# Gathering the first 28 edge tiles from x instead of z, in a graph layer followed by a mixture of experts

## The chip, the core and the metric

The kernel runs on one core of a Trainium2 chip. The metric is the device time of one execution in microseconds (us), and lower is better. The engines are named as the profile names them: PE (TensorE, matmuls), PEld (its weight loads), DVE (VectorE), ACT (ScalarE), POOL (GpSimd) and SP (SyncE). SP and ACT also issue plain transfers, and POOL issues the indirect ones (gathers).

## What is computed

There are 6250 nodes with 256 features, 100,000 edges sorted by destination, and 8 experts with 512 hidden units. Cut to what matters:

```python
def gnn(h, src, dst, W, b):                 # h = layernorm(x)
    msg_sum = segment_sum(h[src], dst)      # one row of h for each edge, summed by destination
    deg = segment_sum(ones, dst)
    agg = msg_sum / maximum(deg, 1)[:, None]
    return concatenate([h, agg], axis=1) @ W.T + b

def ffn(h, ...):                            # h = layernorm(x) of the new x
    xn = layernorm(h) * gamma + beta
    logits = xn @ Wr + br                   # 8 experts, the best 2 of each node are used
    y = sum over the two: softmax weight * (gelu(xn @ W1[e] + b1[e]) @ W2[e] + b2[e])

x = x + gnn(layernorm(x), src, dst, W, b)
x = x + ffn(layernorm(x), ...)
```

## The kernel before

**Weights first, then edges.** The kernel does not sum normalised rows and multiply the sums by W. It multiplies each node row first: `z` is layernorm(x) times the second half of W, with 8 router columns beside it (264 columns, `DZ`), and `u` is x plus the bias plus layernorm(x) times the first half. Both go to device memory (`z_d`, `u_d`). The mean is folded into the weights (`center_weights`, giving `gc`), so a row needs only a product with `gc` and a scale by its own `rstd_x`.

**z stage.** The 49 node tiles of 128 rows are taken in blocks of 4 (`TB`). `load_block` loads x both as rows (`xt`, for the statistics) and as columns (`x_t`, for the products), four blocks ahead. `z_block` takes a block two tiles at a time: `product` makes two PSUM tiles on PE, ACT scales them into `zt` (L284), and SP stores the block in `z_d` (L287). After each pair of tiles it runs one piece of the list `ahead`, which is the statistics of two later node tiles on DVE (`statistics`: L184 and L185), every fourth piece with the deviations of eight tiles (`z_deviations`: a root on ACT and five small DVE instructions). It also runs one entry of the list `steps`. Before the change `steps` has nine entries from block 5 on: constants, the windows of destinations (`place_windows`, `spread_windows`, `place_rows`, `check_windows`), and two checks that the destinations are sorted (`check_order`, L310 and L311).

**u stage.** `u_stages` gives 26 closures. The first 25 each make u of two node tiles: a load of x rows (`xu`, L197), an addition on DVE (L376), two products on PE (L260), four DVE instructions (L383 and L384) and, one closure later, a store (L388).

**Edge stage.** The edges are cut into 784 tiles of 128, 14 tiles (`C`) to a window and 56 windows (`W`). For a tile, POOL gathers 128 rows of `z_d` by `src_i` into one of 28 buffers (`XG`, `xg`), L566, and PE adds them by destination with a one-hot matrix made on DVE (`hot`, L577) into the PSUM tile `pS` (L583). The gather of tile t + 28 is issued behind the matmul of tile t. When a window is complete, `window_done` plans what follows at later tiles: a row that two windows share is passed on by way of device memory (`shared_row`, L589; `keep_sums`, `put_sums`, `share_row`), `window_x1` makes the new x from u and the sums, and after each group of four windows the router, the sorting of tokens and the experts' matmuls are laid between the later edge tiles.

**Order.** Every engine's instructions stand in the order in which the program writes them. `at(t, f)` puts a step behind edge tile t. Before the change six u closures run ahead of tile 0, and the others behind the even tiles 0 to 38. When the last of them has run, the memory of u is freed, the cleared expert inputs (`clear_slots`, L828) and the 16 weight loads on ACT's queue follow. One entry of `loads` (19 in all: expert biases and zeros for device memory, L1094) goes out with each tile from tile 0 on.

Of the kernel before, what the change touches and what calls it, by code (L numbers as in the profile page):

```python
# [17 lines left out]
P = 128  # L18
# [7 lines left out]
GB = 3  # L26
LATE = 40
XG = 28


@with_exitstack
def gnn_ffn_kernel(ctx: ExitStack, tc: tile.TileContext, x, x_cols, src, dst, dst_next, gw, gw_t, gb, gb_cols, gamma, beta,
                   wr, br, w1, b1, w2, b2, out):

# [123 lines left out]
    lanei = early.tile([P, 1], I32, name="lanei", bufs=1)  # L158
    nc.gpsimd.iota(lanei, pattern=[[1, 1]], base=0, channel_multiplier=1)

    def constants():
        nc.vector.tensor_scalar(before, ej, 0.0, None, op0=ALU.is_lt)
        nc.scalar.activation(cols, coli, AF.Copy)
        nc.vector.tensor_copy(lane, lanei)
        nc.vector.tensor_scalar(upper, col, lane, None, op0=ALU.is_gt)
# [110 lines left out]
    def z_block(t0, between):  # L276

        n = min(TB, NT - t0)
        zt = early.tile([P, TB, DZ], F32, name="zt", bufs=3)
        for i in range(0, n, 2):  # L280
            m = min(2, n - i)
            for j in range(m):
                t = t0 + i + j
                nc.scalar.activation(zt[:, i + j, :], product(t, 1), AF.Identity, scale=rstd_x[:, t:t + 1])  # L284
            if i + m == n or t0 >= blocks[-3]:
                i0 = i if t0 >= blocks[-3] else 0
                nc.sync.dma_start(rows_of(z_d, t0 + i0, i + m - i0), zt[:, i0:i + m, :])  # L287
# [7 lines left out]
    src_i = const.tile([P, W, C], I32, name="src_i")  # L295
    dst_i = const.tile([P, W, C], I32, name="dst_i")
    wrong = const.tile([P, 3], F32, name="wrong")

    def load_edges():

        follow = early.tile([P, W, C], I32, name="follow", bufs=1)
        nc.sync.dma_start(dst_i, dst)
        nc.sync.dma_start(src_i, src)
        nc.sync.dma_start(follow, dst_next)
        return follow

    def check_order(follow, i):
        some = slice(i * W // 2, (i + 1) * W // 2)
        down = early.tile([P, W // 2, C], F32, name="down", bufs=1)
# [107 lines left out]

    for t0 in blocks[:4]:
        load_block(t0)
    follow = load_edges()  # L420
    gb_sb = u_pool.tile([P, D], F32, name="gb_sb", bufs=1)
    nc.sync.dma_start(gb_sb, bass.AP(tensor=gb.tensor, offset=gb.offset, ap=[[0, P], [1, D]]))
    placed_rows = []
    steps = [constants, lambda: placed_rows.append(place_windows()), lambda: check_order(follow, 0),
             lambda: spread_windows(placed_rows[0]), lambda: check_order(follow, 1), place_rows, check_windows,
             lambda: None, sum_wrongs]
    router_weights()
    router_columns(1)
    center_weights(1)
# [13 lines left out]
    for t0 in blocks:  # L443
        if t0 + 4 * TB in blocks:
            load_block(t0 + 4 * TB)
        elif t0 == blocks[-3]:
            u_tasks = u_stages()
        z_block(t0, steps if t0 >= blocks[5] else None)
    assert not ahead
    assert not steps  # L450
    router_columns(0)
    wide_b = router_biases()
    center_weights(0)
    add_biases(wide_b)
    zero = u_pool.tile([CAP, D], F32, name="zero", bufs=1)
    nc.vector.memset(zero, 0.0)
    early_pools.close()
# [15 lines left out]
    def weights(pool):  # L473
# [9 lines left out]
    xg = [edges.tile([P, DA], F32, name=f"xg{i}") for i in range(XG)]  # L483
    for g in xg:
        nc.vector.memset(g[:, DZ:], 1.0)


    def variances(G):
# [90 lines left out]

    def add_edges(V, c):  # L580
        if c == 0:
            V.pS = ps.tile([P, DA], F32, name="pS")
        nc.tensor.matmul(V.pS, V.hot[c // HC][:, c % HC, :], xg[(V.g * C + c) % XG],  # L583
                         start=(c == 0), stop=(c == C - 1))

    def shared_row(V):

# [385 lines left out]
    def window_done(V, G, K, t):  # L973

        i = V.g - K.first
        S = LastSteps if K.first + CW == W else Steps
        G.x1.append(V.x1)
        shared_row(V)
        at(t + 1, keep_sums, V)
        at(t + 4, put_sums, V)  # L980
        at(t + 8, share_row, V)
        at(t + S.x1, window_x1, V)
        at(t + S.x1, statistics, G.mv[:, i, :], V.x1[:, :D])
# [24 lines left out]
        at(t + S.rows + 2 + CW * S.apart, load_plans, K)  # L1008
        at(t + S.start, start_experts, K)
# [47 lines left out]
    def new_window(g, V_before):  # L1057
# [2 lines left out]
        hot_tiles(V, 0)  # L1060
        return V

    V = new_window(0, None)
# [201 lines left out]
```

## Time and profile before

| | |
|---|---|
| Runs shown | 1454.48 us median of 3 (1453.49 to 1456.05) |
| The profiled execution | 1454.06 us, of which 1452.1 us are its span |
| Busy in the span | PE 1105.6 us, DVE 699.8, ACT 452.0, POOL 843.4 |
| Granted TensorE clock | 0.877 of full speed, mean |
| z stage | the last scale of z (L284) ends at 66.5 us |
| First and last gather of an edge tile | 70.75 us; 1235.50 us |
| u stage | first L376 at 71.81 us, last at 171.62 us |
| First expert matmul (L849) | 269.3 us |

A row of a timeline gives the start, the duration, the engine, the line, the operation, and in brackets how long the engine had been idle and what released it. "issue" means that the profile shows nothing that the engine was waiting for, and "remote" or "an unknown queue" that it shows an event of a queue it does not know. In a table of windows each stretch has the busy time of every engine with its number of instructions, the granted clock, the mean busy share of the 16 DMA engines, and what they moved in GB/s. A DMA share slightly above 1 comes from overlapping packets.

### The profile page before, as it was taken

The numbers are of one execution on the slowest core, as the hardware profiler recorded it, in microseconds if no ns is written. First come the engines' busy times: TensorE is split into PE (matmuls) and PEld (weight loads), VectorE is DVE, ScalarE is ACT, GpSimd is POOL, SyncE is SP. The second block draws the span as 40 slices with busy tenths as digits, with TensorE's granted clock in tenths as the row PEclk, the third lists the DMA queues.
The fourth block names the chain that finished last, engine by engine and source line by source line (L and its number), as shares of the span: only waits on it lengthen the run. The fifth ranks groups of instructions, "written<-read, shape, count | busy, mean of one in ns | idle before, by whom it ended". The sixth has DMA issues, their size and how long they took to land.

```text
span 1452.1 us, 19064 instructions
## 1 busy us (share of the span) xinstructions
PE 1105.6 (76%) x5236; PEld 913.1 (63%) x5236; DVE 699.8 (48%) x2426; ACT 452.0 (31%) x1264; POOL 843.4 (58%) x892
## 2 busy tenths in 40 slices
PE   7957737486986968697787878898798968968652
PEld 5736625485765757586666657577697756856541
DVE  5735646263544545263453535464453635565223
ACT  2300002342433433333342333334333333425110
POOL 0075666666566666666666666666666666554442
PEclk9979978798898979799897989899899988978866
DMA  9877894445444464545445454444545454555443
GB/s 327 306 249 218 253 323 120 102 131 127 122 127 118 128 124 127 128 130 114 126 130 115 128 119 129 114 134 116 126 131 130 131 122 125 142 161 150 141 149 105
DMA packets 151610, 217.67 MB, mean 150 GB/s; under 512 B 37587, under 2 KB 119158, under 8 KB 151370
## 3 DMA queue, kind: packets, MB, share of 16 engines
q0 software_dynamic: 42768, 118.97, 33.2%
q1 hardware_dynamic: 100394, 87.97, 19.2%
q10 hardware_dynamic: 8336, 9.45, 2.0%
q8 instruction: 44, 0.72, 0.2%
q14 instruction: 68, 0.56, 0.1%
HBM read 163.97 MB, written 52.32 MB: 149 GB/s over the span
## 4 chain that ended last, share of the span: by engine, by line
PE 51%; issue 17%; DVE 8%; another core or an unknown queue 8%; ACT 7%; DMA 4%; SPq 2%; ACTq 2%; POOL 1%; POOLq 0%; DVEq 0%
PE pS L583 17%; PE ph L849 14%; PE py L862 10%; ACT xe L824 4%; PE pm L670 3%; PE ph L892 2%; PE py L910 2%; ACTq L813 1%; ACT hid L854 1%; DVE xg L948 1%; DVE hot L577 1%; DMA u_d<-u_t 1%; DMA xt<-x_dram 1%; PE ph L260 1%
## 5 line engine op out<-in xcount | busy, mean ns | idle before, releaser
L566 POOL DMA_INDIRECT xg<-z_d,src_i x784 | 746.4, 952 | 486.9 <-issue 182.8
L583 PE MATMUL pS<-xg,hot 128*128 128x265 f32 x1568 | 444.4, 417 | 68.9 <-issue 33.7
L583 PEld LDWEIGHTS pS<-xg,hot 128*128 128x128 f32 x1568 | 312.3, 207 | 136.1 <-issue 47.8
L849 PE MATMUL ph<-xe,w_sb 128*128 128x128 f32 x1792 | 259.9, 293 | 103.2 <-issue 94.4
L849 PEld LDWEIGHTS ph<-xe,w_sb 128*128 128x128 f32 x1792 | 244.4, 207 | 126.6 <-issue 109.2
L862 PE MATMUL py<-w_sb,hid 128*128 128x256 f32 x896 | 233.7, 408 | 50.0 <-DVE rows L866 22.4
L862 PEld LDWEIGHTS py<-w_sb,hid 128*128 128x128 f32 x896 | 181.9, 206 | 88.5 <-issue 30.7
L854 ACT ACTIVATE hid<-ph,b_sb 128x128 f32<-128x128 f32 x448 | 126.5, 376 | 334.4 <-remote 190.2
L824 ACT ACTIVATE xe<-xs x448 | 139.4, 311 | 100.3 <-issue 49.9
L577 DVE TENSOR_TENSOR hot<-cols,rel 128x896 f32<-128x896 f32 x112 | 121.1, 1082 | 86.9 <-PE pS L583 56.1
L941 POOL DMA_INDIRECT xg<-y_d,plans x98 | 94.8, 967 | 109.8 <-DVE xg L948 34.0
L866 DVE TENSOR_TENSOR rows<-py,b_sb 128x512 f32<-128x512 f32 x56 | 38.6, 689 | 184.0 <-PE pS L583 63.6
L593 ACT ACTIVATE sums<-pS 128x265 f32<-128x265 f32 x56 | 21.9, 392 | 248.8 <-issue 111.1
L589 DVE TENSOR_TENSOR pS<-pS,row 1x265 f32<-1x265 f32 x55 | 23.5, 427 | 152.9 <-PE pS L583 57.0
L673 ACT ACTIVATE xs<-pm,beta_sb,gamma_sb 128x256 f32<-128x256 f32 x112 | 57.5, 572 | 108.8 <-PE pS L583 41.9
L260 PE MATMUL ph<-gc,x_t 128*128 128x264 f32 (+1 forms) x200 | 59.6, 424 | 25.2 <-DVE u_t L384 13.9
L670 PE MATMUL pm<-to,xn 128*128 128x256 f32 x224 | 63.2, 403 | 16.0 <-ACT xs L673 7.9
L625 DVE SCALAR_TENSOR_TENSOR x<-pS,rdeg,x 128x264 f32<-128x264 f32 x55 | 27.1, 493 | 76.5 <-DMA x<-u_d 47.5
L260 PEld LDWEIGHTS ph<-gc,x_t 128*128 128x128 f32 x200 | 39.0, 203 | 38.3 <-issue 11.9
L670 PEld LDWEIGHTS pm<-to,xn 128*128 128x128 f32 x224 | 43.7, 200 | 26.8 <-ACT xs L673 9.1
L260 PE MATMUL pm<-gc,x_t 128*128 128x264 f32 (+1 forms) x192 | 54.9, 411 | 6.9 <-DVE u_t L384 6.9
L948 DVE SCALAR_TENSOR_TENSOR xg<-xg,plans,xg 128x256 f32<-128x256 f32 (+1 forms) x98 | 46.1, 483 | 22.1 <-DMA xg<-y_d,plans 15.7
(196 smaller groups left out, 825.1 us busy)
## 6 DMA issues: line engine op xcount, KB each, us to landing
y_d<-rows SPq DMA_DIRECT2D x56, 256.0 KB
xg<-z_d,src_i POOLq DMA_INDIRECT x784
w_sb<-w_dram ACTq DMA_DIRECT2D x16, 512.0 KB
sums_d<-sums SPq DMA_DIRECT2D x55, 132.5 KB
x<-u_d SPq DMA_DIRECT2D x55, 132.0 KB
x_d<-x SPq DMA_DIRECT2D x55, 128.0 KB
u_d<-u_t SPq DMA_DIRECT2D x24, 264.0 KB
x_t<-x_cols_dram SPq DMA_DIRECT2D x12, 512.0 KB
```

The costliest lines, as they stand in the source:

```text
L260: nc.tensor.matmul(pz, x_t[:, t, k, :], gc[:, h * KD + k, :n], start=(k == 0), stop=(k == KD - 1))
L566: nc.gpsimd.indirect_dma_start(out=xg[(g * C + c) % XG][:, :DZ], out_offset=None, in_=z_d[:, :], in_offset=bass.IndirectOffsetOnAxis(ap=sr ...
L577: nc.vector.tensor_tensor(hot, col[:, None, :].to_broadcast([P, HC, P]), V.rel[:, c:c + HC, None].to_broadcast([P, HC, P]), op=ALU.is_equal)
L583: nc.tensor.matmul(V.pS, V.hot[c // HC][:, c % HC, :], xg[(V.g * C + c) % XG], start=(c == 0), stop=(c == C - 1))
L670: nc.tensor.matmul(px[:, k, :], G.xn[i][:, k * P:(k + 1) * P], G.one_hot[i], start=True, stop=True)
L673: nc.scalar.activation(xs[:, at:at + 2 * P], px[:, k, :], AF.Identity, bias=beta_sb[:, k:k + 1], scale=gamma_sb[:, k:k + 1])
L824: nc.scalar.activation(xe[:, :, bass.ds(to_at, CAP)], src[:, :, bass.ds(src_at, CAP)], AF.Copy)
L849: nc.tensor.matmul(ph[:, i, a * SH:(a + 1) * SH], w1_sb[:, U.e + a, k, c * P:(c + 1) * P], xe[:, k, at:at + SH], start=(k == 0), stop=(k = ...
L854: nc.scalar.activation(U.hid[:, c, a * SH:(a + 1) * SH], ph[:, i, a * SH:(a + 1) * SH], AF.Gelu, bias=b1_sb[:, U.e + a, c:c + 1])
L862: nc.tensor.matmul(U.py[:, h, :], U.hid[:, c, h * P:(h + 1) * P], w2_sb[:, U.e + h, c, :], start=(c == 0), stop=(c == KH - 1))
L941: nc.gpsimd.indirect_dma_start(out=V.y2[r], out_offset=None, in_=y_d[:K.batch.end_row, :], in_offset=bass.IndirectOffsetOnAxis(ap=plans[:c ...
L948: nc.vector.scalar_tensor_tensor(V.o, V.y2[r], plans.bitcast(F32)[:count, n, 2 + r:3 + r], V.o, op0=ALU.mult, op1=ALU.add)
```

## The change

The first two windows (`RAW` is 28 // 14) take rows of `x` instead of rows of `z_d`. Their 28 gathers stand at the very start of the program, behind a small load of their own indices. While z is made, DVE takes the statistics of the 3584 gathered rows (`raw_statistics`, `raw_deviations`), and ACT scales the rows in place (`scale_raw`). The PSUM sums of these two windows are then sums of scaled x rows; they are copied out, transposed, multiplied by `gc` and put back (`take_raw_sums`, `turn_raw_sums`, `multiply_raw_sums`), and the window's later steps are planned up to 4 tiles later.

`steps` has 18 entries and starts at block 3. It now also holds `router_columns(0)`, `router_biases`, `center_weights(0)` and `add_biases`, which stood behind the z stage. The load of `follow`, both order checks and `sum_wrongs` move behind the z stage, to tiles 6, 12 and 18. `u_stages`, with its first three loads of x, is called behind the z stage instead of at block 10, and no u closure runs ahead of tile 0, so the 26 closures stand behind the even tiles 0 to 50.

```diff
+RAW = XG // C
...
+    nc.sync.dma_start(src_i[:, :RAW], src[:, :RAW])
+    xg = [edges.tile([P, DA], F32, name=f"xg{i}") for i in range(XG)]
+    for t in range(RAW * C):
+        nc.gpsimd.indirect_dma_start(
+            out=xg[t][:, :D], out_offset=None, in_=x[:, :],
+            in_offset=bass.IndirectOffsetOnAxis(ap=src_i[:, t // C, t % C:t % C + 1], axis=0))
     def constants():
+        for g in xg:
+            nc.vector.memset(g[:, D:DZ], 0.0)
+            nc.vector.memset(g[:, DZ:], 1.0)
...
             if between:
-                between.pop(0)()
+                for f in between.pop(0):
+                    f()
+    def raw_statistics(some):
+        for t in some:
+            statistics(mv_e[:, t // C, t % C, :], xg[t][:, :D])
+    def raw_deviations(g):
+        a = small.tile([P, C], F32, name="var_eps_e", bufs=1)
+        nc.vector.tensor_scalar(a, mv_e[:, g, :, 1], EPS, None, op0=ALU.add)
+        rsqrt(rstd_e[:, g, :], a, root(a, C, C), C, C)
+    def scale_raw(some):
+        for t in some:
+            nc.scalar.activation(xg[t][:, :D], xg[t][:, :D], AF.Identity, scale=rstd_e[:, t // C, t % C:t % C + 1])
     def load_edges():
-        follow = early.tile([P, W, C], I32, name="follow", bufs=1)
         nc.sync.dma_start(dst_i, dst)
-        nc.sync.dma_start(src_i, src)
+        nc.sync.dma_start(src_i[:, RAW:], src[:, RAW:])
+    def load_follow():
+        follow = u_pool.tile([P, W, C], I32, name="follow", bufs=1)
         nc.sync.dma_start(follow, dst_next)
...
-    steps = [constants, lambda: placed_rows.append(place_windows()), lambda: check_order(follow, 0),
-             lambda: spread_windows(placed_rows[0]), lambda: check_order(follow, 1), place_rows, check_windows,
-             lambda: None, sum_wrongs]
+    steps = [[constants], [some(raw_statistics, 0, 0, 4)],
+             [lambda: placed_rows.append(place_windows())], [some(raw_statistics, 0, 4, 4)],
+             [lambda: spread_windows(placed_rows[0])], [some(raw_statistics, 0, 8, 4)],
+             [place_rows], [some(raw_statistics, 0, 12, 2), lambda: raw_deviations(0)],
+             [check_windows], [some(raw_statistics, 1, 0, 4), some(scale_raw, 0, 0, 3)],
+             [some(raw_statistics, 1, 4, 3), some(scale_raw, 0, 3, 3)],
+             [some(raw_statistics, 1, 7, 3), some(scale_raw, 0, 6, 3)],
+             [some(raw_statistics, 1, 10, 4), lambda: raw_deviations(1), some(scale_raw, 0, 9, 3)],
+             [lambda: router_columns(0), some(scale_raw, 0, 12, 2)],
+             [lambda: wide_b.append(router_biases()), some(scale_raw, 1, 0, 3)],
+             [lambda: center_weights(0), some(scale_raw, 1, 3, 3)],
+             [lambda: add_biases(wide_b[0]), some(scale_raw, 1, 6, 4)],
+             [some(scale_raw, 1, 10, 4)]]
...
-        elif t0 == blocks[-3]:
-            u_tasks = u_stages()
-        z_block(t0, steps if t0 >= blocks[5] else None)
+        z_block(t0, steps if t0 >= blocks[3] else None)
-    router_columns(0)
-    wide_b = router_biases()
-    center_weights(0)
-    add_biases(wide_b)
+    u_tasks = u_stages()
+    follow = load_follow()
...
+    def take_raw_sums(V):
+        V.raw = work.tile([P, D], F32, name="raw", bufs=1)
+        nc.scalar.activation(V.raw, V.pS[:, :D], AF.Copy)
+    def turn_raw_sums(V):
+        pt = ps.tile([P, KD, P], F32, name="pm")
+        for k in range(KD):
+            nc.tensor.transpose(pt[:, k, :], V.raw[:, k * P:(k + 1) * P], ident)
+        V.raw_t = work.tile([P, KD, P], F32, name="raw_t", bufs=1)
+        nc.scalar.activation(V.raw_t, pt, AF.Copy)
+    def multiply_raw_sums(V):
+        for k in range(KD):
+            nc.tensor.matmul(V.pS[:, :DZ], V.raw_t[:, k, :], gc[:, KD + k, :DZ], start=(k == 0), stop=(k == KD - 1))
...
-        shared_row(V)
-        at(t + 1, keep_sums, V)
+        more = 0
+        if V.g < RAW:
+            take_raw_sums(V)
+            at(t + 1, turn_raw_sums, V)
+            at(t + 3, multiply_raw_sums, V)
+            more = 4
+        at(t + more, shared_row, V)
+        at(t + 1 + more, keep_sums, V)
...
-    for g, c in edge_tiles[:XG]:
-        gather(g, c)
-    for _ in range(6):
-        u_tasks.pop(0)()
+    at(6, check_order, follow, 0)
+    at(12, check_order, follow, 1)
+    at(18, sum_wrongs)
```

More of the change, by code (lines that the diff above doesn't have):

```diff
@@ L159, in gnn_ffn_kernel @@
     nc.gpsimd.iota(lanei, pattern=[[1, 1]], base=0, channel_multiplier=1)
+    src_i = const.tile([P, W, C], I32, name="src_i")
+    dst_i = const.tile([P, W, C], I32, name="dst_i")
+    nc.sync.dma_start(src_i[:, :RAW], src[:, :RAW])
[4 more added lines that the diff above has]
+            in_offset=bass.IndirectOffsetOnAxis(ap=src_i[:, t // C, t % C:t % C + 1], axis=0))
     def constants():
+        for g in xg:
+            nc.vector.memset(g[:, D:DZ], 0.0)
+            nc.vector.memset(g[:, DZ:], 1.0)
         nc.vector.tensor_scalar(before, ej, 0.0, None, op0=ALU.is_lt)
@@ L290, in z_block @@
             if between:
-                between.pop(0)()
-    src_i = const.tile([P, W, C], I32, name="src_i")
-    dst_i = const.tile([P, W, C], I32, name="dst_i")
+                for f in between.pop(0):
+                    f()
+    mv_e = edges.tile([P, RAW, C, 2], F32, name="mv_e")
+    rstd_e = edges.tile([P, RAW, C], F32, name="rstd_e")
+    def raw_statistics(some):
[8 more added lines that the diff above has]
+            nc.scalar.activation(xg[t][:, :D], xg[t][:, :D], AF.Identity, scale=rstd_e[:, t // C, t % C:t % C + 1])
     wrong = const.tile([P, 3], F32, name="wrong")
     def load_edges():
-        follow = early.tile([P, W, C], I32, name="follow", bufs=1)
         nc.sync.dma_start(dst_i, dst)
-        nc.sync.dma_start(src_i, src)
+        nc.sync.dma_start(src_i[:, RAW:], src[:, RAW:])
+    def load_follow():
+        follow = u_pool.tile([P, W, C], I32, name="follow", bufs=1)
         nc.sync.dma_start(follow, dst_next)
@@ L308, in check_order @@
         some = slice(i * W // 2, (i + 1) * W // 2)
-        down = early.tile([P, W // 2, C], F32, name="down", bufs=1)
+        down = u_pool.tile([P, W // 2, C], F32, name="down", bufs=1)
         nc.vector.tensor_tensor(down, dst_i[:, some], follow[:, some], op=ALU.is_gt)
@@ L419, in gnn_ffn_kernel @@
         load_block(t0)
-    follow = load_edges()
+    load_edges()
     gb_sb = u_pool.tile([P, D], F32, name="gb_sb", bufs=1)
@@ L423, in gnn_ffn_kernel, with some @@
     placed_rows = []
-    steps = [constants, lambda: placed_rows.append(place_windows()), lambda: check_order(follow, 0),
-             lambda: spread_windows(placed_rows[0]), lambda: check_order(follow, 1), place_rows, check_windows,
-             lambda: None, sum_wrongs]
+    def some(f, g, first, n):
+        return lambda: f(range(g * C + first, g * C + min(first + n, C)))
+    wide_b = []
+    steps = [[constants], [some(raw_statistics, 0, 0, 4)],
[11 more added lines that the diff above has]
+             [some(scale_raw, 1, 10, 4)]]
     router_weights()
@@ L481, in weights @@
         return w1_sb, w2_sb, parts
-    xg = [edges.tile([P, DA], F32, name=f"xg{i}") for i in range(XG)]
-    for g in xg:
-        nc.vector.memset(g[:, DZ:], 1.0)
     def variances(G):
@@ L977, in window_done @@
         G.x1.append(V.x1)
-        shared_row(V)
-        at(t + 1, keep_sums, V)
[L980 to L983, printed above, removed]
+        more = 0
[6 more added lines that the diff above has]
+        at(t + 1 + more, keep_sums, V)
+        at(t + 4 + more // 2, put_sums, V)
+        at(t + 8 + more // 4, share_row, V)
+        at(t + S.x1 + more, window_x1, V)
+        at(t + S.x1 + more, statistics, G.mv[:, i, :], V.x1[:, :D])
         if i < CW - 1:
@@ L1061, in new_window @@
         return V
+    now = 0
     V = new_window(0, None)
     edge_tiles = [(g, c) for g in range(W) for c in range(C)]
-    for g, c in edge_tiles[:XG]:
-        gather(g, c)
-    for _ in range(6):
-        u_tasks.pop(0)()
+    at(6, check_order, follow, 0)
+    at(12, check_order, follow, 1)
+    at(18, sum_wrongs)
     for index in range(W // CW):
```

## The prediction

> **What bounds the kernel now.** I read the part of the page on the chain of waits first, then a table of windows over the start, then the timelines of DVE, POOL and PE there. The whole chain is half PE, and a good part of it is engines that resume late for no reason the profile shows:
>
> ```profile
> PE 51%; issue 17%; DVE 8%; another core or an unknown queue 8%; ACT 7%; DMA 4%; SPq 2%; ACTq 2%; POOL 1%; POOLq 0%; DVEq 0%
> ```
>
> POOL is 1% of it, so the 784 gathers, though 746 us long together, do not set the end. From edge tile 74 on the orders of before and after are nearly the same, so the change is worth what it moves the time of that tile. Until then three stages follow each other: z (to 66.5), u (to 171), the router of the first four windows (to 220). In the windows below the columns are PE, PEld, DVE, ACT, POOL, clock, DMA share and GB/s:
>
> ```profile
> 30.00:40.00 10.00, 8.50 (x37) 6.98 (x38) 6.09 (x25) 5.07 (x14) 0.00 (x0) 1.00 1.07 384
> 40.00:50.00 10.00, 8.66 (x40) 7.06 (x39) 8.90 (x42) 3.62 (x9) 0.00 (x0) 1.00 1.07 388
> 50.00:60.00 10.00, 8.15 (x38) 6.31 (x37) 8.62 (x43) 3.94 (x10) 0.00 (x0) 1.00 0.88 309
> 70.00:80.00 10.00, 9.03 (x39) 6.78 (x38) 8.73 (x35) 0.00 (x0) 7.12 (x8) 1.00 0.69 204
> 90.00:100.00 10.00, 2.15 (x4) 1.17 (x4) 0.66 (x2) 0.00 (x0) 7.56 (x9) 0.57 0.62 208
> ```
>
> The z stage has no free resource where the change puts its work: to 50 us the DMA engines are full (share 1.07), and from 40 to 60 DVE is busy 8.6 to 8.9 of 10 us. At 90 to 100 us, in the u stage, everything but POOL stands still. The timelines of DVE and PE show these two places:
>
> ```profile
> 30.90 0.43 DVE L184 BATCH_NORM_STATS2 st<-xt 128x6 f32<-128x256 f32 x1 [1.89 <-DMA xt<-x_dram]
> 31.46 0.39 DVE L184 BATCH_NORM_STATS2 st<-xt 128x6 f32<-128x256 f32 x1
> 31.99 0.40 DVE L184 BATCH_NORM_STATS2 st<-xt 128x6 f32<-128x256 f32 x1
> ...
> 94.84 0.17 DVE L383 TENSOR_TENSOR u_t<-ph,gb_r 128x8 f32<-128x8 f32 x1 [8.90 <-remote]
> 103.94 0.17 DVE L383 TENSOR_TENSOR u_t<-pm,gb_r 128x8 f32<-128x8 f32 x1 [8.40 <-issue]
> 113.06 0.17 DVE L383 TENSOR_TENSOR u_t<-ph,gb_r 128x8 f32<-128x8 f32 x1 [7.83 <-issue]
> ...
> 150.60 1.08 PE L260 MATMUL ph<-gc,x_t 128*128 128x272 f32 x4
> 153.33 1.08 PE L260 MATMUL ph<-gc,x_t 128*128 128x272 f32 x4
> ...
> 219.64 0.66 PE L643 MATMUL pm<-both,ones 128*128 128x64 f32 x2 [17.38 <-DVE rdeg L623]
> ```
>
> One row's statistics cost DVE 0.53 us a tile (31.99 - 31.46), and tile 20's wait for their load. DVE resumes late three times, about 25 us in all, while POOL issues its first 29 gathers back to back. The last row is tile 74: PE waits 17 us for the router's chain on DVE.
>
> **The change part by part.** I carry five times forward.
>
> *Gathers (early).* The POOL timeline gives one every 1.25 us (0.95 + 0.30), so from about 3 us, when a small index load has landed (gamma's took from 1.26 to 3.69), 28 x 1.25 = 35 us, done at 38. POOL is idle there. The bytes are not free: 28 x 128 x 1 KB = 3.67 MB. Two rows price them. q0, the gathers' queue, moved 118.97 MB in 33.2% of 1452.1 us, 247 GB/s: 14.9 us. The z stage moves 384 GB/s: 9.6 us. The Trainium skill (DMA: Bandwidth & Descriptors, Specifications) says that transfers from 512 B a descriptor run at line rate, which speaks for the second; the x rows of the node tiles that make the 384 are 1 KB as well, while q0's rows are 1056 B. I take 9.6, less 1.0 for `follow` (392 KB at 384 GB/s), which leaves this stage: x for tile 20 comes 8.6 us later, 30.9 + 8.6 = **39.5**. Bounds: 5 (in the first 10 us the DMA share was 0.81) and 14.
>
> A rule speaks against gathers here. The row: from 70 to 80 us POOL issued 8 gathers at that pitch beside a DVE busy 8.73 us. The Trainium skill (SBUF — State Buffer, Who interferes with whom) says that DVE in a two-port mode shuts GpSimd out for the whole instruction, and gives 3100 ns for a 620 ns transfer: five times. On 28 gathers, as an estimate, 28 x 5.05 = 141 us, and z would wait for them. By the row it is 0. I take the row: the same section exempts instructions with one SBUF input outside such modes, and DVE's work in the first 38 us is mostly L184.
>
> *DVE in z.* `steps` starts with the pair of tiles 12 and 13, whose pieces are the statistics of tiles 20 and 21. From tile 20 to the deviations of tiles 40 to 47, DVE took from 30.90 to 60.40, 29.5 us, of which 2.3 were waits for x. Out go the checks: 2 x 1.05 (45.49 to 46.53). In come 28 x 0.53 = 14.8 of statistics, two sets of deviations at 1.4 (41.99 to 43.36), and 56 small memsets, 0.8 (28 took 0.40). 27.2 - 2.1 + 14.8 + 2.8 + 0.8 = 43.5, all ahead of those deviations: 39.5 + 43.5 = **83.0** instead of 60.4. Nothing covers it: z of 40 and on cannot be scaled before.
>
> *The end of z.* Behind them ACT has 9 z tiles at 0.38 (60.57, 60.95) and the last 16 scalings; for one, as wide and from SBUF, I take 0.37. 3.4 + 5.9 = 9.3 us (6.1 before, when PE set the pace): last z at **92.3** instead of 66.5. The other 12 scalings lie beside DVE's work on an ACT busy 3.6 to 5 of 10 us. The router columns and biases (PE, 65.7 to 68.9) are covered by the same ACT time; uncovered they cost 3.
>
> *Start of u.* SP's queue is written in order: the first load of x for u stands behind the last z store now, not 8 us ahead. Store 0.4, load 0.6, landing 2.4: the first L376 at **95.7** instead of 71.8. The `follow` load behind them costs SP 0.4.
>
> *u stage.* 25 pairs, now with two edge tiles each from the start. Before, six pairs ran alone; tile 52 came at 181.2 (the run of tiles 49 to 55 begins at 179.04, 0.73 each). In its clean stretches a pair takes 2.73 us (150.60, 153.33), all PE. From the L376 at 116.91 to that at 129.48, four pairs, it is 3.14; to the last at 171.62, fifteen, 3.65, with windows ending between and waits of 1 to 4 us for u's stores. I take 3.14 for seven pairs and 3.65 for eighteen: 87.7, tile 52 at **183.4**, 2.2 later. In this the 25 us of late resumes are gone, with the 28 gathers in a row that went beside them; now POOL is in step with PE's matmuls. Gather 28 (needed at tile 28, 45 us on) and both checks (2 us of DVE) are hidden.
>
> *To tile 74.* The four clears of the expert inputs (L828, 2.165 us each) follow 12 tiles later. Three stood ahead of the first router's chain; three now stand in it (tiles 58, 63, 68): 6.5 us of DVE, of which its late resumes there (10.6 us) may hide some: I take 4 (0 to 6.5). The weights also start 12 tiles later; the wait of 5.65 us for the shared row at 187 to 192 moves from window 3 to window 4: 0 (-6 to +6). Raw sums: per window two ACT copies (0.39), two transposes and four passes of 0.42 on PE, some 1.5 us beside a PE with gaps: 1 for both. A gather lead of 28 tiles instead of some 23 is worth nothing, as PE waits for DVE at tile 74 either way.
>
> **Sum** against the profiled 1454.06 (span 1452.1 and 2.0 around it): 2.2 + 4 + 1 = 7.2, so 1461.3; that execution is 0.4 below the median of the runs shown, so **1461**. Said as a balance: z gives away 25.8, the u stage gives back 21.7 of the 23.9 lost at its start.
>
> **The rivals.**
>
> *A: the u stage runs at PE's pace, faster.* If 25 pairs take 2.73, tile 52 comes at 95.7 + 68.3 = 164.0, 17 earlier; with 5 behind it the kernel takes 1442. For it: five pairs in a row did so, and there are no back-to-back gathers. Against: 0.80 MB of u, x and gathers a pair is 293 GB/s, above the 256 of 150 to 160 us. It decides at 80.5 / 25 = 3.22 us a pair: below that the kernel is faster.
>
> *B: the late resumes come again.* They were on DVE alone, with no DMA backlog behind 95 us, and I do not know their cause. If it is DVE's place in its program and not the burst, they cost 25 more: 1486. That the three came with the burst and ended behind it speaks against; that such waits are a quarter of the whole chain, for.
>
> *C: the gathers' transfers are hidden.* If ring shares favour x, d is near 0, DVE fills its own 2.3 us, and z ends 17 later, not 26: 1453, no change. DMA shares of 0.97 to 1.07 from 10 to 50 us speak against.
>
> **How the numbers follow.** My forecast 0.42 (1453 to 1469 by its own bounds), A 0.26, B 0.20, C 0.12. The range leaves out the better end of A and the worst of B: 1438 to 1486. About 0.2%, 2.9 us, is what can be told from no change here. Faster: nearly all of A and some of C, 0.28. Same: most of C and the low edge of the forecast, 0.13. Slower: the rest, 0.59.
>
> **What would show it.** Right: POOL gathers from 3 to 38 us; the first L184 on tile 20 near 39; DVE over 9 of 10 us from 40 to 80; the last L284 near 92; no 8 us gaps at L383; the last L376 near 184; the four L828 inside the first router's chain. Wrong: the last L284 before 80, or a pitch of L376 under 3.2 us.

## The result and the profile after

The changed kernel takes 1461.9 us (median), the kernel before 1455.6 on the same chip: a ratio of 1.0035 with a 95% interval of 1.0021 to 1.0049. It is slower by 6.3 us (5.1 by the ratio), and the predicted time, 1461, is met. The profiled execution took 1463.5 us, of which 1461.6 are its span. The two profiled executions differ by 9.5 us of span, so some 3 us of what the two traces show is only these two executions.

In the window table of the changed kernel the columns after the length are busy us of PE, PE's weight loads, DVE, ACT and POOL with the instructions that began, then PE's clock, DMA share and GB/s:

```profile
20.00:30.00 10.00, 2.25 (x5) 1.17 (x4) 2.31 (x12) 0.57 (x2) 7.57 (x9) 0.68 1.05 380
30.00:40.00 10.00, 2.13 (x4) 1.18 (x4) 2.16 (x10) 0.48 (x1) 5.90 (x7) 0.50 0.76 267
60.00:70.00 10.00, 7.22 (x32) 5.51 (x30) 8.99 (x40) 2.15 (x6) 0.00 (x0) 1.00 1.00 339
80.00:90.00 10.00, 6.03 (x28) 4.85 (x26) 9.00 (x39) 3.81 (x12) 0.00 (x0) 0.84 0.23 78
120.00:130.00 10.00, 10.00 (x45) 8.36 (x44) 8.41 (x22) 0.00 (x0) 6.39 (x7) 1.00 0.90 261
```

POOL's gathers end in the second row, at 37.7 us, as forecast, and from 60 to 90 us DVE is busy 8.6 to 9.0 of 10 us. What was not forecast is PE at 2.25 and 2.13 of 10 us and DVE at 2.31 and 2.16: beside the gathers nearly everything stands still. From 30 to 40 us the DMA is no longer full, so waiting for bytes is not all of it. The timeline (start, duration, then the wait ahead of it) says what else; the ACT row is the last scaling of z:

```profile
24.85 0.18 DVE L190 RECIPROCAL rstd_x<-root 128x4 f32<-128x4 f32 x1 [7.95 <-issue]
29.86 0.18 DVE L201 BATCH_NORM_AGGREGATE mv<-st 128x2 f32<-128x6 f32 x1 [2.31 <-remote]
37.56 0.18 DVE L201 BATCH_NORM_AGGREGATE mv<-st 128x2 f32<-128x6 f32 x1 [3.00 <-issue]
41.76 0.18 DVE L201 BATCH_NORM_AGGREGATE mv<-st 128x2 f32<-128x6 f32 x1 [1.59 <-remote]
46.89 0.39 DVE L200 BATCH_NORM_STATS2 st<-xt 128x6 f32<-128x256 f32 x1
...
101.96 0.46 ACT L300 ACTIVATE zt<-ph,rstd_x 128x264 f32<-128x264 f32 x1
...
107.03 0.68 DVE L406 TENSOR_TENSOR u_t<-xu,gb_sb 128x512 f32<-128x512 f32 x1
...
185.92 0.42 DVE L406 TENSOR_TENSOR u_t<-xu,gb_sb 128x256 f32<-128x256 f32 x1
```

These are the late resumes of the kernel before, in another place. A late resume is a wait that ends microseconds after everything that the instruction needs is there, for no reason that the trace shows. L201 needs only the six numbers a row that DVE itself wrote one instruction earlier, and yet it starts 2.3 or 3.0 us late, with a releaser that the trace cannot name. In the kernel before, three waits of some 8 us stood in the u stage, beside the row of back-to-back gathers from 70 to 106 us. Now that row is in z, and the waits stand there: from 17 us (14 after the first gather) to 42. Tile 20's statistics begin at 46.89, the last z scaling ends at 102.42, and the first L406 (the addition of u, L376 before) is at 107.03. From there to the 25th L406 (185.92) it is 78.9 us, and the longest wait of DVE in it is 3.2 us; in the kernel before it was 99.8 (71.81 to 171.62).

At tile 74 PE waits for the router's chain on DVE, as in the prediction's last step (219.64 us before):

```profile
225.18 0.66 PE L694 MATMUL pm<-both,ones 128*128 128x64 f32 x2 [16.74 <-DVE rdeg L674]
```

### The profile page after: what moved, and what is told of

Read it like the earlier page. It is cut to its first block, busy times and chain, and to the rows that moved or that the text cites. A ratio compares the mean times of both kernels' runs of the same rounds, so it can differ in the third digit from the quotient of the medians.

```text
span 1461.6 us, 19235 instructions
## 1 busy us (share of the span) xinstructions
PE 1111.6 (76%) x5248; PEld 918.2 (63%) x5248; DVE 715.1 (49%) x2522; ACT 465.2 (32%) x1298; POOL 842.8 (58%) x892
## 4 chain that ended last, share of the span: by engine, by line
PE 50%; issue 18%; ACT 7%; DVE 6%; another core or an unknown queue 5%; DMA 3%; ACTq 2%; POOL 1%; SPq 0%; POOLq 0%; DVEq 0%
PE pS L619 17%; PE ph L900 14%; PE py L913 8%; ACT xe L875 4%; PE pm L721 3%; PE ph L943 2%; PE py L961 2%; ACTq L864 2%; ACT hid L905 1%; PE pm L276 1%; PE ph L276 1%; DVE xg L999 1%; POOL xg L602 1%; DMA xg<-y_d,plans 1%
## 5 line engine op out<-in xcount | busy, mean ns | idle before, releaser
L602 POOL DMA_INDIRECT xg<-z_d,src_i x756 | 718.5, 950 | 490.8 <-issue 165.5
L619 PE MATMUL pS<-xg,hot 128*128 128x265 f32 x1568 | 448.3, 419 | 63.2 <-issue 33.5
L619 PEld LDWEIGHTS pS<-xg,hot 128*128 128x128 f32 x1568 | 313.2, 208 | 135.0 <-issue 61.4
L900 PE MATMUL ph<-xe,w_sb 128*128 128x128 f32 x1792 | 266.0, 299 | 114.8 <-issue 101.0
L900 PEld LDWEIGHTS ph<-xe,w_sb 128*128 128x128 f32 x1792 | 249.3, 212 | 137.9 <-issue 113.4
L913 PE MATMUL py<-w_sb,hid 128*128 128x256 f32 x896 | 227.1, 398 | 44.4 <-DVE rows L917 22.2
L913 PEld LDWEIGHTS py<-w_sb,hid 128*128 128x128 f32 x896 | 177.3, 200 | 79.4 <-issue 42.8
L276 PE MATMUL ph<-gc,x_t 128*128 128x264 f32 (+1 forms) x200 | 61.0, 432 | 21.7 <-ACT zt L300 10.8
L721 PE MATMUL pm<-to,xn 128*128 128x256 f32 x224 | 59.1, 386 | 10.1 <-ACT xs L724 7.9
L999 DVE SCALAR_TENSOR_TENSOR xg<-xg,plans,xg 128x256 f32<-128x256 f32 (+1 forms) x98 | 46.2, 483 | 24.3 <-DMA xg<-y_d,plans 11.4
```

The source lines that it names most:

```text
L276: nc.tensor.matmul(pz, x_t[:, t, k, :], gc[:, h * KD + k, :n], start=(k == 0), stop=(k == KD - 1))
L602: nc.gpsimd.indirect_dma_start(out=xg[(g * C + c) % XG][:, :DZ], out_offset=None, in_=z_d[:, :], in_offset=bass.IndirectOffsetOnAxis(ap=sr ...
L721: nc.tensor.matmul(px[:, k, :], G.xn[i][:, k * P:(k + 1) * P], G.one_hot[i], start=True, stop=True)
L900: nc.tensor.matmul(ph[:, i, a * SH:(a + 1) * SH], w1_sb[:, U.e + a, k, c * P:(c + 1) * P], xe[:, k, at:at + SH], start=(k == 0), stop=(k = ...
L913: nc.tensor.matmul(U.py[:, h, :], U.hid[:, c, h * P:(h + 1) * P], w2_sb[:, U.e + h, c, :], start=(c == 0), stop=(c == KH - 1))
L999: nc.vector.scalar_tensor_tensor(V.o, V.y2[r], plans.bitcast(F32)[:count, n, 2 + r:3 + r], V.o, op0=ALU.mult, op1=ALU.add)
```

## Which row to compare: the gather of the same edge tile

POOL issues all gathers in one order, so the start of the gather of edge tile T can be read as a clock for the whole edge loop. It is gather T of z in the kernel before, and gather T - 28 of z in the changed one. In POOL's timelines tile 28's is the first of these lines for before, and the second for the changed kernel; the last two are tile 783's, the last of each:

```profile
106.35 0.95 POOL L566 DMA_INDIRECT xg<-z_d,src_i  x1 [0.30 <-issue]
```
```profile
107.82 0.94 POOL L602 DMA_INDIRECT xg<-z_d,src_i  x1 [70.09 <-DMA follow<-dst_next_dram]
```
```profile
1235.50 0.95 POOL L566 DMA_INDIRECT xg<-z_d,src_i  x1 [0.30 <-issue]
```
```profile
1247.27 0.95 POOL L602 DMA_INDIRECT xg<-z_d,src_i  x1 [0.30 <-issue]
```

Although z ends 36 us later, tile 28's gather comes only 1.5 us later, because in the kernel before POOL issues 28 other gathers behind z first, from 70.75 to 106.35. That is the balance of the change. At tile 100 the difference is -1.1, at tile 128 it is +6.1 (the first router's chain lies between), at the last tile +11.8. Behind the last gather the kernel takes 214 to 218 us in each of the six traces on this kind of chip, and 154 to 159 in each of the eight on the other kind (next section), so in every kernel here the end follows the last gather within some 5 us.

## Chips that differ

The runs below came on three chips, called B, C and D; D may be the chip of the pair above (A) again. B and C differ from A far more than any two kernels here do. The same kernel before took:

| chip | runs | kernel before, median us | of its chain "issue" and unknown |
|---|---|---|---|
| A | the pair above | 1455.6 | 25% |
| B | e1 to e4 | 1210.7 | not traced; 4 to 5% in e1 to e4 |
| C | e5 to e8 | 1213.1 | 4% |
| D | e9 to e12 | 1458.6 | not traced; 20 to 25% in e9 to e12 |

So ratios are taken against before on the same chip; where a run is set against the changed kernel of another chip, it is by their two ratios. On A the chain's issue and unknown shares are 25% of 1452.1 us, 363; on C 4% of 1212.8, 49. The spans differ by 239, so the late resumes are large enough for the whole difference between the chips. That they are its only cause is not shown: other shares differ too (DMA 4% on A, 26% on C), and so does the mean granted clock (0.877 and 0.933). In the first 220 us DVE has no wait over 1.5 us without a named releaser in any of the eight traces on B and C; PE has one to three a trace, up to 4.3 us. The chain of the kernel before on C, and that of the changed kernel on C:

```profile
PE 57%; DMA 26%; DVE 9%; issue 4%; POOL 2%; ACT 1%; SPq 1%; ACTq 0%; POOLq 0%; DVEq 0%
```
```profile
PE 51%; DMA 23%; DVE 10%; issue 4%; ACT 2%; POOL 1%; SPq 1%; ACTq 0%; POOLq 0%; DVEq 0%
```

Getting such chips was luck: they show the change almost without late resumes.

## Experiments

There are three theories of z's delay: the *row* (back-to-back gathers make the engines resume late), the *bytes* (3.67 MB hold back x) and the *place* (late resumes belong to a spot in the program). Then there are two theories of what pays the delay back: PE's *sum of work* in the u stage, or POOL's *gather stream*. The code below is cut to the lines that matter.

**e1, one gather.**

```
-    for t in range(RAW * C):
-        nc.gpsimd.indirect_dma_start(
-            out=xg[t][:, :D], out_offset=None, in_=x[:, :],
...
+    nc.gpsimd.indirect_dma_start(
+        out=xf, out_offset=None, in_=x[:, :],
...
-            statistics(mv_e[:, t // C, t % C, :], xg[t][:, :D])
+            statistics(mv_e[:, t // C, t % C, :], xf)
-            nc.scalar.activation(xg[t][:, :D], xg[t][:, :D], AF.Identity, ...
+            nc.scalar.activation(xg[t][:, :D], xf, AF.Identity, ...
```

> One gather at the start instead of 28; the statistics and scalings of all 28 edge tiles read that one tile, so DVE, ACT and PE do the same work (27 gathers and their 3.5 MB are left out, and the sums of the first two windows are other numbers). Gathers are what delays z, as a burst or as bytes: no wait over 1.5 us of DVE behind its own instruction, tile 20's statistics near 32 us (46.9 in the changed kernel), last z scale near 32 + 45 + 9 = 86 (102), and if all of it is passed on some 1447 us. Place in the program (late resumes without any gather): tile 20 near 46, last z near 101, 1461.

Tile 20's statistics begin at 28.53, the last z ends at 83.17, and the ratio is 0.9959 (0.9945 to 0.9973). The changed kernel on C (e6) has 35.96 and 89.33, so on chips like B and C the gathers cost z 6.2 to 7.4 us. The expected 32 and 1447 were for chip A.

**e2, short rows.** As e1, and the 28 gathers behind it, of 256-byte rows (other rows of x, which nothing reads).

```
     for t in range(RAW * C):
         nc.gpsimd.indirect_dma_start(
-            out=xg[t][:, :D], out_offset=None, in_=x[:, :],
+            out=xg[t][:, :D // 4], out_offset=None, in_=x.rearrange("n (q d) -> (n q) d", q=4)[:, :],
```

> The same work as with one gather, and behind it the 28 gathers again, back to back, but of rows of 256 bytes instead of 1 KB, which nothing but the much later scalings waits for (0.9 MB instead of 3.7). Burst of gathers: as in the changed kernel, DVE and ACT resume late from 24 to 45 us, tile 20's statistics near 46, last z scale near 101, 1461. Bytes: a quarter of 15.9 us is left, tile 20 near 35, last z near 89, 1450.

Tile 20's statistics begin at 30.24, the last z ends at 84.84, and the ratio is 0.9996 (0.9980 to 1.0012). The first of these lines is tile 20's in e1, the second in e2:

```profile
28.53 0.43 DVE L200 BATCH_NORM_STATS2 st<-xt 128x6 f32<-128x256 f32 x1 [1.93 <-DMA xt<-x_dram]
```
```profile
30.24 0.43 DVE L204 BATCH_NORM_STATS2 st<-xt 128x6 f32<-128x256 f32 x1 [2.71 <-DMA xt<-x_dram]
```

All gathers are there, in a row, beside DVE, and a quarter of the bytes costs 1.7 us, about a quarter of the 7.4. So on this kind of chip z is delayed by bytes. At the end e2 lies 4.5 us over e1 (by the ratios, give or take 2.6), more than the 1.7 of z; where the rest goes its trace does not show. The run also bears on the rule that the prediction weighed (the Trainium skill, SBUF — State Buffer, Who interferes with whom): DVE's statistics kept their length (0.39 to 0.43) and the row kept its pitch (POOL 7.56 of 10 us from 10 to 30), so a lock cost at most these 1.7 us, not 141. That agrees with the section's exemption for instructions with one SBUF input, on which the prediction relied; no run tests the two-port case by itself.

**e3, paced gathers.** Eight at the start, then one (from tile 24, two) behind each pair of z, for which POOL waits.

```
+    gather_raw(range(8))
...
+                nc.gpsimd.tensor_copy(pace, zt[:, i, 0:1])
+                n_raw = 1 if t0 + i < 24 else 2
+                gather_raw(raw_left[:n_raw])
```

> The same 28 gathers of the same bytes, spread out: 8 at the start, then 1 (later 2) behind each pair of z tiles, for which POOL waits. Burst: the late resumes go, tile 20's statistics near 38 us, last z scale near 92 to 94, 1453. Bytes: by tile 20 some 18 of the 28 have come, so 0.65 of the delay is left: tile 20 near 42, last z near 98, 1458. Place in the program: 46, 102, 1462.

Tile 20's statistics begin at 32.55, the last z ends at 86.33, and the ratio is 1.0016 (1.0004 to 1.0029), against the changed kernel's 1.0024 on C. z gains 3.0 us; at the end the two cannot be told apart. On a chip without late resumes the run says nothing on them.

**e4, no statistics.** DVE's statistics and deviations of gathered rows are left out.

```
     def raw_statistics(some):
-        for t in some:
+        for t in []:
             statistics(mv_e[:, t // C, t % C, :], xg[t][:, :D])
     def raw_deviations(g):
...
+        pass
...
+            nc.scalar.activation(xg[t][:, :D], xg[t][:, :D], AF.Identity, scale=rstd_x[:, 0:1])
```

> All 28 gathers, scalings and matmuls stay, DVE's 28 statistics and two sets of deviations for the gathered rows are left out (the scalings take another factor). By the prediction's sum DVE loses 14.8 + 2.8 = 17.6 us: deviations of tiles 40 to 47 end near 75 (92.2 in the changed kernel), last z near 85. If the end of z is passed on in full: 1445. If the u stage is set by its transfers and takes most of it back, as its bound from before (3.65 us a pair) would have it: 1456.

Tile 20's statistics begin at 36.31, the deviations of tiles 40 to 47 end at 68.11, the last z ends at 77.89, and the ratio is 0.9939 (0.9925 to 0.9953). With the statistics (e6, on C) the times are 35.96, 79.94 and 89.33. So 17.6 us of DVE's work are worth 11.4 at z's end, since behind tile 20 DVE then waits 2.8 us for x and 2.1 us more for roots of ACT, and those 11.4 go through to the end nearly whole (the ratios are 0.0085 apart, 10.3 us).

**e5, before again, and e6, after again, on C.**

> The kernel before, unchanged, for its trace on the chip of these runs: the four runs so far ran on a chip where it takes 1210.7 us, not 1455.6, and where waits of the chain put down to 'issue' or an unknown source are 4 to 5% of the span instead of 23 to 25%. If the late resumes belong to the chip and not to the program: chain with some 5% of issue, no 8 us gaps in the u stage at 86 to 113 us, first u product near 72 us and tile 52 near 160. If they belong to the burst of 28 gathers: the gaps are there here too, tile 52 near 180.

> The changed kernel, unchanged, on the chip of these runs. Without late resumes z loses what the prediction's sum gives it (tile 20's statistics near 37 to 39 us, deviations of tiles 40 to 47 near 81, last z near 90), and the u stage no longer has 25 us of late resumes to give back: 25 pairs at some 3.1 us, tile 52 near 172, so 8 to 12 us over before (ratio 1.007 to 1.010). If the gain in the u stage came from the two early windows and not from absent late resumes: ratio 1.0035 as on the first chip.

Before: tile 20's statistics begin at 28.88, the last z ends at 64.63, the last pair of u comes near 147, and DVE has no late resume beside its row of gathers; the single run took 1214.8. After: the ratio is 1.0024 (1.0011 to 1.0036). This is what the z stage beside the gathers looks like there, to be set against the rows of A above:

```profile
20.00:30.00 10.00, 7.45 (x33) 5.77 (x32) 4.41 (x20) 2.85 (x8) 7.56 (x9) 1.00 1.05 379
30.00:40.00 10.00, 6.61 (x18) 4.87 (x17) 5.85 (x76) 1.90 (x5) 5.89 (x7) 0.67 1.06 386
...
35.96 0.43 DVE L200 BATCH_NORM_STATS2 st<-xt 128x6 f32<-128x256 f32 x1 [3.63 <-DMA xt<-x_dram]
```

The POOL column is the same, but PE is busy 7.45 us and DVE 4.41, and DVE's wait has a name: it is for x. So late resumes do not come from the place in the program. I had expected the change to lose 8 to 12 us on a chip without late resumes, as the u stage has none to give back. z does end 24.7 us later, tile 74's router matmul comes 11.6 later and the first expert matmul 15.5 later (222.89, 238.37), but the kernel loses only some 3 us by the ratio. Tile 74 on C, before and after:

```profile
189.01 0.66 PE L643 MATMUL pm<-both,ones 128*128 128x64 f32 x2 [10.67 <-DVE rdeg L623]
```
```profile
200.64 0.66 PE L694 MATMUL pm<-both,ones 128*128 128x64 f32 x2 [9.70 <-DVE rdeg L674]
```

The clock of gathers says why. The table has the difference to the kernel before for the gather of tile T, in us:

| T | 28 | 60 | 78 | 128 | 228 | 428 | 628 | 783 |
|---|---|---|---|---|---|---|---|---|
| C, changed kernel | -10.4 | -2.5 | +1.8 | +0.8 | +1.9 | +2.2 | +2.0 | +2.4 |
| C, half (e7) | -6.1 | -7.0 | -6.2 | -7.1 | -6.0 | -5.8 | -5.7 | -5.5 |
| A, changed kernel | +1.5 | +0.5 | +0.4 | +6.1 | +6.0 | +9.4 | +9.6 | +11.8 |

On C a difference that stands at tile 78 is still there within 1 us or so at 783, 880 us later. From its 200th gather of z to the last one POOL issues one every 1.25 us, with no wait to speak of, in the changed kernel as in the one before. These are the first and the last gather of z on C, before, and then the same two of the changed kernel; the last ones start 0.30 us behind the end of the one ahead:

```profile
68.63 1.13 POOL L566 DMA_INDIRECT xg<-z_d,src_i  x1 [66.78 <-DMA xu<-x_dram]
...
1053.50 0.95 POOL L566 DMA_INDIRECT xg<-z_d,src_i  x1 [0.30 <-issue]
```
```profile
94.72 0.94 POOL L602 DMA_INDIRECT xg<-z_d,src_i  x1 [57.00 <-DVE u_t L406]
...
1055.88 0.95 POOL L602 DMA_INDIRECT xg<-z_d,src_i  x1 [0.30 <-DMA xg<-z_d,src_i]
```

The sum on C: the stream starts 26.1 us later (94.72 instead of 68.63), has 28 gathers less (28 x 1.2525 = 35.1), and its first 100 gathers take 14.3 us over their pitch instead of 3.3. Of these 14.3 POOL waits 7.2 for PE's edge matmuls, which free the buffers, and 3.7 for DVE in the u stage. 26.1 - 35.1 + 11.0 = +2.0, against +2.4 at the last gather. On A the same three terms are 37.1 - 35.1 + 10.3 = +12.3, against +11.8.

**e7, half.** Only the first 14 edge tiles take x.

```
-RAW = XG // C
+RAW = 1
-             [check_windows], [some(raw_statistics, 1, 0, 4), some(scale_raw, 0, 0, 3)],   # and so on
+             [check_windows], [some(scale_raw, 0, 0, 3)],
+    for g, c in edge_tiles[RAW * C:XG]:
+        gather(g, c)
```

> The first 14 edge tiles gather rows of x, not 28; the next 14 gather z behind its last store, in a row, while u begins. By the prediction's terms it takes 14 x 0.53 + 1.4 = 8.8 us of DVE, 4.8 us of transfers ahead of tile 20 and 5.6 us of scalings from z: last z some 12 us earlier than in the changed kernel, the u stage the same: ratio to the changed kernel 0.990. If a row of 14 gathers beside u makes the engines resume late: 10 us or more of it are lost again, 0.998.

The last z ends at 77.78, 11.6 us earlier than in the changed kernel, as the prediction's terms had it. The ratio is 0.9960 (0.9944 to 0.9976), so half is faster than both kernels; to the changed one it is 0.9936 (0.9960 / 1.0024), where 0.990 had been expected. The stream starts 14.3 us earlier than in the changed kernel, has 14 gathers more (17.5 us), and loses 3.1 us in its first 100 gathers instead of 14.3: -14.3 + 17.5 - 11.2 = -8.0, and the table has -7.9 at the last tile (-5.5 against +2.4). DVE did not resume late.

**e8, clears on ACT.**

```
-        nc.vector.memset(xe[:, :, part * size:SC if part == 3 else (part + 1) * size], 0.0)
...
+        nc.scalar.activation(piece, xs[:, zero_at:zero_at + 1, None].to_broadcast([P, KD, piece.shape[2]]), AF.Copy)
```

> The changed kernel with the four clears of the expert inputs on ACT (a copy of a zero column) instead of DVE's memsets. The prediction's term of 4 us (0 to 6.5) for clears inside the first router chain: tile 74's router matmul and the end 4 to 6 us earlier, ratio to the changed kernel 0.996. If DVE's chain waits for the edge tiles or for PE there, and not the other way round: no change, 1.000; if ACT's copies hold up the window sums behind them: 1 to 2 us slower.

The ratio is 1.0020 (1.0001 to 1.0040); the changed kernel's is 1.0024. Counted from the last z, tile 74's router matmul comes 2.3 us earlier (109.0 behind it instead of 111.3), and at the end no gain can be told. On a chip with late resumes it was not tried.

**e9, 28 later gathers left out.**

```
-                if t + XG < len(edge_tiles):
+                if t + XG < len(edge_tiles) and not (t >= 200 and t % 16 == 0 and t < 648):
```

> The changed kernel with 28 of the later gathers of z left out, every 16th between tiles 200 and 648 (those edge tiles use the rows that lie in the buffer). On the last two chips POOL issued its gathers every 1.2525 us from about the 50th to the last, whatever z had lost. If POOL's queue is the bound behind the u stage: 28 x 1.25 = 35 us less, ratio to before 1.002 - 0.029 = 0.973. If PE sets the pace and gathers are hidden (on a chip with a pitch of 1.49 us a gather, as the first one was): 0 to 5 us, ratio 1.000.

It ran on D, where gathers come every 1.50 us on average and PE and DVE show late resumes as on A. The ratio is 0.9790 (0.9774 to 0.9806). Against the changed kernel's 1.0035 on A that is 35.7 us, give or take 3, which is 1.28 us a gather. I had expected nearly nothing where the pitch is 1.49, and was wrong: POOL's work counts whole there too, though POOL is 1% of that trace's chain. POOL's timeline has rows of gathers at 1.25, and between them waits, most of those with a name for PE's matmuls; PE itself waits 87.5 us at two of its lines (L900 and L619) without a named releaser between 300 and 1200 us. From the 200th gather of z on, the time over the pitch is 132 us, nearly that of the changed kernel on A (138), so it is the 28 pitches that went. No run separates fewer gathers from fewer late resumes beyond that. The timeline at one place:

```profile
408.75 0.94 POOL L602 DMA_INDIRECT xg<-z_d,src_i  x1 [1.94 <-PE pS L619]
410.00 0.95 POOL L602 DMA_INDIRECT xg<-z_d,src_i  x1 [0.30 <-issue]
411.25 0.95 POOL L602 DMA_INDIRECT xg<-z_d,src_i  x1 [0.30 <-remote]
412.51 0.95 POOL L602 DMA_INDIRECT xg<-z_d,src_i  x1 [0.30 <-issue]
414.87 0.94 POOL L602 DMA_INDIRECT xg<-z_d,src_i  x1 [1.42 <-PE ph L900]
```

**e10, half with two u pairs ahead.**

```
+        elif t0 == blocks[-3]:
+            u_tasks = u_stages()
+    for _ in range(2):
+        u_tasks.pop(0)()
```

> The kernel with 14 gathered tiles of x, and in it the loads for u are issued ahead of the last three blocks of z again, and two u pairs run ahead of the first one-hot tiles, while the last stores of z land. PE stood still for 5.5 us there and two pairs are some 5.5 us of the u stage: if they fit into it, 4 to 5 us less, ratio to before 0.992. If z's tail is set by DVE and ACT, and the two pairs only go ahead of what they would have followed: 0.996 as without it.

The ratio is 0.9967 (0.9951 to 0.9984), no better than half alone (e11 below). The first pair of u comes 5.9 us earlier than in e11, and the last one 2.7 earlier; but the first gather of z comes 1.1 later (82.99, 81.90), and the last one too (1236.1, 1235.0). That fits the stream: an earlier u was worth nothing.

**e11, half again, on D.**

> The kernel with 14 gathered tiles of x once more, beside the others on the same chip: 0.996 to before if what it saves (8.8 us of DVE, 4.8 of transfers, 5.6 of scalings in z, and 14 of POOL's 28 early gathers kept) holds on this chip too; on a chip with late resumes a row of 14 gathers beside u may cost some 10 us: 1.000 to 1.003.

The ratio is 0.9943 (0.9917 to 0.9969): on this kind of chip too half beats the kernel before, and the changed kernel's 1.0035. It is also the only run that shortens the row on a chip with late resumes. With 14 gathers from 2.8 to 20 us DVE has one long late resume in z, and tile 20's statistics begin at 33.07 (46.9 with 28 in e9 and e12 on the same chip). From 81.9 to 105.6 the other 14 and five that follow make a row of 19 without a wait, and DVE has its next long one there, in the u stage:

```profile
22.02 0.18 DVE L190 RECIPROCAL rstd_x<-root 128x4 f32<-128x4 f32 x1 [4.34 <-issue]
...
106.31 0.17 DVE L413 TENSOR_TENSOR u_t<-ph,gb_r 128x8 f32<-128x8 f32 x1 [12.85 <-remote]
```

**e12, six u pairs alone again.**

```
+    for _ in range(6):
+        u_tasks.pop(0)()
```

> The changed kernel with the first six u pairs alone ahead of the edge tiles again, as before the change. If PE's sum of work sets the u stage, its order is worth nothing: ratio to before 1.002. If POOL's start counts: the first matmul, and with it the first gather of z, comes some 14 us later, and some 10 us of the 14 that POOL loses in the first 100 gathers are given back: 3 to 6 us slower, 1.006.

The ratio is 1.0069 (1.0052 to 1.0086), 5 us over the changed kernel's on A (give or take 3). PE has the same work; the first gather of z comes 10.3 us later than in e9 (118.59, 108.27), whose order up to there is the changed kernel's. PE's sum of work alone would have given no change. But tile 74's router matmul is 5.8 us later than in e9 as well (223.95, 218.15), so this run does not tell the stream from the time of tile 74. e9 does, as its gathers are left out far behind that tile.

## Why the prediction was right, and where it was not

The time and the sign are right, and the time is met by luck: two terms were off by some 10 us each and cancelled, and the one that explains the balance was put at nothing. By its own steps:

*Gathers on POOL*: right. They end at 37.7 with the pitch of 1.25, and DVE's work beside them cost next to nothing (e2). The 3100 and 620 ns that the prediction weighs stand in another section of the page that it names (A bandwidth-pool intuition that's wrong), where they are for a DVE copy; its 141 us was never a forecast.

*Tile 20's statistics at 39.5*: 46.89. Its 8.6 us for the transfers are about the right size: bytes cost 7.1 on C. What was missed on A is the late resumes, 7.4 us at this point. The prediction knew them, and took them as gone "with the 28 gathers in a row that went beside them"; the row had only moved. Rival B had them return for 25 us, if they belonged to DVE's place in its program; they returned with the row, in z, as 19.7 us of waits from 17 to 42 us, of which tile 20 shows 7.4 over the forecast.

*DVE in z, 43.5*: 45.3 on A, 44.0 on C. Right, though leaving the statistics out again saves less than the 17.6 put in for them: it is 31.8 then (e4), 12.2 less, as DVE waits for x and for ACT instead.

*Tail of z, 9.3*: 10.3 on A, 9.4 on C, with the scalings at 0.40 instead of 0.37. *Start of u, 3.4 behind it*: 4.6; two one-hot tiles of 1.08 us go ahead of it on DVE, which the prediction left out. The last z and the first u pair are 10.1 and 11.3 us later than forecast, 7.4 of them from tile 20's start.

*u stage, 87.7*: from the first L406 to tile 52 it is 77.5, 3.10 a pair by the prediction's count instead of 3.51. The mis-sized term is the 3.65 taken for eighteen pairs: the first seven took 25.3 us (22.0 forecast), the other eighteen up to tile 52 took 52.2, 2.90 each. A pitch under 3.2 was the prediction's own sign of being wrong. It came without the faster kernel that rival A drew from it, because A counts from a first u pair 11 us earlier. On C, without late resumes, from the first L406 to the 25th it is 76.8 us before and 77.7 after.

*Tile 52 at 183.4*: 184.5 (the run of tiles 49 to 55 begins at 183.11, 0.47 each). It came out by luck, as the sum of the two errors.

*Clears, +4, and raw sums, +1*: on A the router matmul comes 5.5 later and the gather of tile 128 6.1, near the 7.2 that 2.2, 4 and 1 make; on C no worth of the clears can be told at the end (e8). For A it stays open.

*"A gather lead of 28 tiles instead of some 23 is worth nothing, as PE waits for DVE at tile 74 either way"*: wrong, and this is the term that was missing. At tile 74 PE does wait for DVE, but behind it POOL's stream sets the pace on C (e6 to e8), and on D 28 gathers taken out far behind tile 74 are worth 35.7 us (e9). So "the change is worth what it moves the time of that tile" fails: on C tile 74 moves by 11.6 us and the last gather by 2.4. The first step went wrong in the same way: "POOL is 1% of it, so the 784 gathers ... do not set the end" takes the chain's share for the bound. On C POOL is 1 to 2% of the chain, and from its 200th gather of z on it never rests over 0.32 us between two of them. That the u stage gives back 21.7 us came out on A (99.8 - 78.9 = 20.9 from the first L406 to the 25th), but it is not what carries the balance: on C the u stage gives back nothing, and the kernel loses no more. What the change pays for the 35 us is a stream that starts 26 us (C) to 37 us (A) later, and some 10 us more over the pitch in its first 100 gathers.

## What to carry to other kernels

Where one queue issues work in a fixed order and at a fixed pitch to the end, compare the two kernels at the same item of that queue; a stage's gain or loss counts only as far as it moves the queue's start, its number of items or its waits. A small share of the chain does not show that an engine sets no pace: look for a pitch without waits too. Work given early to an idle engine is paid for where its followers land: here these are the statistics on DVE and the bytes ahead of x, and half of it was better than all. And a stall that moves with what goes beside it isn't gone: ask where that is now.

## What the runs showed of the hardware

Late resumes depend on the chip: the same kernel before takes 1452.1 us of span with 25% of its chain in issue and unknown waits, or 1212.8 with 4%. On A and D the longest ones of DVE in z and u come beside rows of gathers, and they moved with the row in each kernel. DVE's first long wait begins 14.0 us behind the first gather of the row (A, changed), 15.2 (A, before), 11.6 (e11's second row). They go on some 4 us past the row's end in the changed kernel. In z a row of 14 leaves one long wait of 4.3 us (e11), where a row of 28 leaves 19.7 us of them (A, changed); in the u stage a row of 19 leaves one of 12.9 (e11). A gather's issue took 0.95 us and its pitch in a row was 1.25 on every chip. Why A and D have late resumes and B and C hardly any, and by what path a gather on POOL could delay a wait between two instructions of DVE, no run here shows. One gather alone, paced gathers and rows of short gathers were run only on B, so whether they keep the late resumes away stays open, and so does whether the row causes them or only goes beside them.
